# A two-layer image model on one core: the first and last rounds of a software pipeline in a written order, and scan matrices built by matrix products

## The chip, the cores and the metric

The kernel runs on one core of a Trainium2 chip. The core has a matrix engine (TensorE, PE in the profile; its weight loads are PEld), a vector engine (DVE), a scalar engine (ACT), GpSimd (POOL) and a queue for transfers (SyncE, SP). Each engine takes its instructions strictly in the order of the program, and waits for the others through semaphores. A matrix product can only write to PSUM, and has to be moved from there by DVE or ACT. The metric is the device time of one execution in microseconds (us); less is better.

## The reference

The input is 32 images of 56 x 56 pixels with 96 channels, in float32. Two layers follow each other; each adds a mixer and then a feed-forward network (FFN) to the running image, and each part begins with a normalization over the channels:

```python
x = x + _L0_conv_ref(_ln_c(x), ...)      # shifted 7x7-window attention, 3 heads of 32
t = _to_tokens(x)
t = t + _L0_ffn_ref(_ln_t(t), ...)       # 96 -> 384 -> 96, operands rounded to 8-bit floats
x = _from_tokens(t, x)
x = x + _L1_conv_ref(_ln_c(x), ...)      # gate * scan along the rows' axis, 192 channels
t = t + _L1_ffn_ref(_ln_t(t), ...)       # a second such FFN
```

The scan of layer 1 is a linear recurrence along one image axis with 16 states per channel:

```python
def step(state, u_w):
    st = state * A + u_w[..., None] * B
    y = jnp.sum(st * C, axis=-1) + S * u_w * D
    return (st, y)
```

As it is linear, its output is for each channel a fixed lower-triangular Toeplitz matrix (56 x 56) applied to a line of 56 pixels. The entries of the matrix are the channel's "taps": the sums over the states of C A^n B, with D added to the first.

## The kernel before

The images are cut into 128 blocks, four to an image; a block is 14 image rows of 56 pixels (seven tiles of 2 x 56 tokens and 96 channels) and lives in one of 14 buffers `xb` while everything is done on it. What is done to a block is some 90 steps with short names. In the order of a block's way:

| steps | what they do | engine |
|---|---|---|
| `LD` | load the block, six or nine transfers | SP |
| `sa`, `ma`, `na`; `ta`, `ea` | statistics, mean off, times root; transposes and their copy | DVE; PE, ACT |
| `q`, `k`, `v`; `eq`, `ek`, `ev` | projections (tiles `qk`, `pv`) and their copies | PE; ACT |
| `sc`; `st0`-`st2`; `ex0`-`ex2`; `av` | scores; scale and bias; exp; times values | PE; DVE; ACT; PE |
| `rc`, `an`; `tro`, `eo`; `pr`, `ad` | normalize; transpose, copy; output projection, add | DVE; PE, ACT; PE, DVE |
| `sf`, `mf`, `nf`, `tf`, `ef` | normalization of FFN 0 | DVE, POOL, POOL, PE, ACT |
| `hf`, `xf`, `rf`, `cf` (0-2); `yf`, `zf`, `bf`, `kf` | FFN 0: hidden product, copy, bias and relu, 8-bit cast; output product, copy, bias, add | PE, ACT, DVE, POOL/DVE; PE, ACT, DVE, POOL |
| `se`, `me`, `ne`, `te`, `xe` | normalization of the scan mixer | DVE, POOL, POOL, PE, ACT |
| `pu`, `th`, `uc` (0-3) | gate and expansion products; tanh; copy to `u` | PE; ACT; ACT |
| `SC`, `GA` (0-5) | scan as products with `toep` over the blocks of a window; gating | PE; DVE |
| `gt`, `eg`; `so`, `as` | transposes, copies; output product, add | PE, ACT; PE, DVE |
| `sg` ... `kg` | FFN 1, as FFN 0, with `cg` and `kg` on DVE | |
| `ST` | store the block, six or nine transfers | SP |

The eight steps `R0` to `R7` compute on DVE, in one pass, the inverse roots of all four normalizations that have statistics waiting; a normalization between `s` and `n` needs a full pass.

The order of the work is a text, `PIPELINED`: a list of entries `name:lag`. In round t the entry does its step on block t − lag, so the steps of about 14 blocks lie interleaved. The rounds run from t = 0 to 141; in the first ones only the entries of low lag have a block, in the last ones only those of high lag. `in_order` fixes this order on every engine. `banks` hands out four PSUM slots of two banks each, first in, first out; `EMPTIES` says which steps empty a slot.

Work that is done once (the preparation) is placed by hand around the first rounds: `prepare_attention` before round 0, `prepare_bias` after it, `prepare_hidden` and `prepare_matrices` around round 1, `prepare_mixer` before round 2. Much of it are memsets on POOL (L159 to L209, L267 and L439 to L475). `prepare_taps` (L276 to L301) raises the powers of A on DVE, weighs and sums them and transposes the taps on PE (tile `tapsT`). `load_toep` writes the taps 56 times to DRAM (L310) and reads them back in 12 transfers, shifted by one per line (L318), into the gate's second buffer `gts[1]`; `turn_toep` copies that, reordered, into `toep` before the first scan.

Before all this, `bounded` derives a flag from the attention's weights and position table; every engine reads it (L1065, L1066) and branches to the pipelined program or, where it does not hold, to a plain one (`IN_TURN`). With these inputs the pipelined one runs.

Of the kernel before, what the change touches and what calls it, by code (L numbers as in the profile page):

```python
# [17 lines left out]
C = 96  # L18
# [49 lines left out]

IN_TURN = (
    "LD:0 sa:0 R0:0 R1:0 R2:0 R3:0 R4:0 R5:0 R6:0 R7:0 ma:0 na:0 ta:0 ea:0 q:0 eq:0 k:0 ek:0 v:0 ev:0 any:0 "  # L70
# [8 lines left out]

EMPTIES = (  # L80
    "ea:ta eq:q ek:k ev:v st0:sc st1:sc st2:sc an:av eo:tro ad:pr ef:tf xf0:hf0 xf1:hf1 xf2:hf2 zf:yf xe:te "
# [6 lines left out]
def kernel(  # L88
# [81 lines left out]
    load(0)  # L170
    b1r = zeros(64, "bias1r")
    for iy in range(WS):
        nc.sync.dma_start(
# [7 lines left out]
    load(1)  # L181
# [36 lines left out]

    u = const.tile([128, EH, HW], F32, name="u")
# [8 lines left out]

    def bounded():
# [30 lines left out]
    abc = stage(C, 6 * NS).rearrange("p (n h s) -> p n h s", n=3, h=2)  # L260
    for n, src in enumerate((ssm_a, ssm_b, ssm_c)):
        nc.sync.dma_start(abc[:, n], src.rearrange("(h p) s -> p h s", p=C))
    a_t, b_t, c_t = abc[:, 0], abc[:, 1], abc[:, 2]
    d_t = const.tile([C, 2], F32, name="ssm_d")
    nc.sync.dma_start(d_t, ssm_d.rearrange("(h p) -> p h", p=C))
    for n in range(2, PRELOADED):
        nc.gpsimd.memset(xbufs[n], 0.0)  # L267
        load(n)
    powers = stage(C, 2 * HW * NS)
    powers = powers.rearrange("p (h t s) -> p h t s", h=2, s=NS)  # L270
    taps = stage(C, 4 * HW).rearrange("p (h t) -> p h t", h=2)
    taps_t = stage(2 * HW, E)
    ne = EH // 2

    def prepare_taps():
        nc.vector.tensor_copy(powers[:, :, 0, :], b_t)  # L276

        n = 1
        while n < HW:
# [8 lines left out]
            if n < HW:  # L288
                nc.vector.tensor_tensor(a_t, a_t, a_t, ALU.mult)
        nc.vector.tensor_tensor(powers, powers, c_t[:, :, None, :].to_broadcast([C, 2, HW, NS]), ALU.mult)  # L290
        nc.vector.memset(taps, 0.0)
        nc.vector.tensor_reduce(taps[:, :, HW:], powers, op=ALU.add, axis=AX.X)
        nc.vector.scalar_tensor_tensor(taps[:, :, HW], d_t, float(NS), taps[:, :, HW], op0=ALU.mult, op1=ALU.add)

        nc.vector.tensor_scalar_mul(taps, taps, 0.5)
        pt = banks("tapsT")
        for h in range(2):
            nc.tensor.transpose(pt[0 : 2 * HW, 0, h * C : (h + 1) * C], taps[:, h, :], ident[0:C, 0:C])

        for e0, src in ((0, 0), (ne, 3 * ne), (2 * ne, 2 * ne), (3 * ne, ne)):  # L300
            nc.vector.tensor_copy(taps_t[:, e0 : e0 + ne], pt[0 : 2 * HW, 0, src : src + ne])  # L301
# [817 lines left out]
```

## Time and profile before

| | us |
|---|---|
| runs shown: 3128.44, 3133.34, 3138.48; median | 3133.34 |
| the profiled execution's own time | 3137.61 |
| its span, first to last instruction | 3135.6 |
| PE, DVE, ACT, POOL busy | 3053.4, 2681.6, 2339.4, 1408.4 |
| start of R0 in rounds 2, 3, 6, 15 | 46.31, 66.03, 121.30, 305.62 |
| start of R0 in rounds 123, 130, 137 | 2845.04, 3007.13, 3098.08 |
| last `GA` ends; last `kg` ends | 3095.7; 3127.5 |

The profile is of one execution. "Busy" counts an engine's instructions, without waiting; a line such as L896 is a line of the kernel. In a row of the timeline stand the start, the duration, the engine, the line, the operation, output and input tiles, and in brackets the idle time before it with what ended it. The row "PEclk" and the clock in the stage tables are the clock that was granted to TensorE as a share of full speed. From round 18 (R0 at 375.51) to round 123 a round takes (2845.04 − 375.51) / 105 = 23.52 us.

### The profile page before, as it was taken

To read this page: it belongs to the slowest core of one execution; us is meant where nothing else is said; L and a number is where in the kernel's file an instruction comes from. 1 tells how busy PE (TensorE), PEld (TensorE's weight loads), DVE (VectorE), ACT (ScalarE), POOL (GpSimd) and SP (SyncE) were. 2 spreads that over 40 slices of the span, in tenths; PEclk is the share of its full clock that TensorE was granted. 3 is DMA by queue.
4 is the path that set the end of the run, shared out by engine and by line. 5 is a ranking of instruction groups with operands and counts; after the bars stand their busy time and mean duration, and the time that the engine had idled before them with its cause. 6 is when DMAs were issued, how large, how long until landed. Compare 5 with 4: busy or idle time off the path is not lost.

```text
span 3135.6 us, 180306 instructions
## 1 busy us (share of the span) xinstructions
PE 3053.4 (97%) x80164; PEld 2472.0 (79%) x80164; DVE 2681.6 (86%) x7213; ACT 2339.4 (75%) x4610; POOL 1408.4 (45%) x1091
## 2 busy tenths in 40 slices
PE   4999999999999999999999999999999999999996
PEld 3788888888888888888888888888888888888875
DVE  6778888888888888888888888888888888888886
ACT  1677777777777777777777777777777777777774
POOL 4454444444444444444444444444444444444441
PEclk8899999999999999999999999999999999999998
DMA  6100111111111111111111111111111111111001
GB/s 135 30 4 19 27 34 27 27 34 27 27 35 27 27 31 31 27 34 27 27 34 27 27 35 27 27 34 27 27 35 27 27 34 27 27 34 27 23 22 34
DMA packets 232640, 97.09 MB, mean 31 GB/s; under 512 B 225292, under 2 KB 231854, under 8 KB 231854
## 3 DMA queue, kind: packets, MB, share of 16 engines
q1 hardware_dynamic: 228410, 84.40, 11.7%
q8 instruction: 633, 10.37, 1.4%
q10 hardware_dynamic: 3444, 1.06, 0.2%
q14 instruction: 153, 1.25, 0.1%
HBM read 42.05 MB, written 43.35 MB: 27 GB/s over the span
## 4 chain that ended last, share of the span: by engine, by line
PE 96%; DVE 2%; POOL 1%; ACT 1%; issue 0%; SPq 0%; DMA 0%; ACTq 0%; POOLq 0%; DVEq 0%
PE pu L896 20%; PE so L992 10%; PE qk L616 9%; PE scan L939 6%; PE av L738 6%; PE pv L635 6%; PE ph_f L815 5%; PE s L658 5%; PE pr L793 5%; PE ph_g L815 4%; PE py_f L849 4%; PE py_g L849 4%; PE gt L217 3%; PE tr_a L217 2%; PE tr_f L566 2%; PE tr_e L217 2%
## 5 line engine op out<-in xcount | busy, mean ns | idle before, releaser
L896 PE MATMUL pu<-weg,xs 128*64 128x192 f32 x7168 | 663.3, 330 | 4.6 <-ACT xs L882 3.7
L535 DVE BATCH_NORM_STATS2 stats<-xb 128x6 f32<-128x192 f32 x2048 | 585.3, 346 | 1.7 <-POOL xb L871 1.6
L896 PEld LDWEIGHTS pu<-weg,xs 128*64 128x64 f32 x7168 | 485.6, 137 | 76.7 <-ACT xs L882 6.6
L839 POOL CAST hq<-h_f 128x784 fp8e5<-128x784 f16 x256 | 248.7, 972 | 497.6 <-DVE h_f L833 497.6
L555 POOL TENSOR_TENSOR xn_f<-xc_f,roots 128x672 fp8e5<-128x672 f32 x128 | 244.6, 1911 | 467.8 <-DVE roots L517 467.8
L871 POOL TENSOR_TENSOR xb<-xb,y_f 128x672 f32<-128x672 f32 x128 | 224.5, 1754 | 378.9 <-DVE y_f L867 375.6
L917 ACT COPY u<-pu 128x384 f32<-128x384 f32 (+1 forms) x512 | 236.4, 462 | 186.9 <-PE pu L896 186.9
L992 PE MATMUL so<-wso,gT 128*64 128x96 f32 x7168 | 326.7, 249 | 4.6 <-ACT gT L982 4.6
L827 ACT CAST h_f<-ph_f 128x784 f16<-128x784 f32 x384 | 318.2, 829 | 12.1 <-PE ph_f L815 12.1
L827 ACT CAST h_g<-ph_g 128x784 f16<-128x784 f32 x384 | 314.4, 821 | 13.6 <-PE ph_g L815 11.9
L992 PEld LDWEIGHTS so<-wso,gT 128*64 128x64 f32 x7168 | 302.6, 138 | 13.8 <-ACT gT L982 5.2
L541 POOL TENSOR_TENSOR xc_f<-xb,stats 128x672 f32<-128x672 f32 x128 | 174.8, 1365 | 288.0 <-DVE stats L535 170.5
L616 PE MATMUL qk<-xw,wqkv 128*32 128x196 f32 (+1 forms) x3072 | 296.2, 390 | 0.0
L687 DVE SCALAR_TENSOR_TENSOR pT<-s,bias 128x196 f32<-128x196 f32 (+1 forms) x512 | 213.5, 459 | 88.2 <-PE s L658 74.3
L628 ACT COPY qk<-qk 128x784 f32<-128x784 f32 (+1 forms) x256 | 166.1, 650 | 148.3 <-PE qk L616 146.5
L849 PEld LDWEIGHTS <-hq 128*128 128x128 fp8e5 x5376 | 252.7, 98 | 26.9 <-DVE hq L839 8.5
L959 DVE SCALAR_TENSOR_TENSOR gt<-gt,scan 128x448 f32<-128x448 f32 (+1 forms) x632 | 234.7, 428 | 35.4 <-PE scan L939 32.4
L700 ACT ACTIVATE pT<-pT 128x392 f32<-128x392 f32 x384 | 194.8, 528 | 74.2 <-DVE pT L687 74.0
L586 DVE TENSOR_TENSOR xb<-so,xb 128x384 f32<-128x384 f32 (+1 forms) x256 | 118.0, 502 | 152.4 <-PE so L992 152.4
L911 ACT ACTIVATE gt<-pu 128x384 f32<-128x384 f32 (+1 forms) x512 | 230.6, 450 | 18.0 <-PE pu L896 8.6
L616 PEld LDWEIGHTS qk<-xw,wqkv 128*32 128x32 f32 (+1 forms) x3072 | 120.6, 119 | 136.9 <-issue 127.6
L738 PEld LDWEIGHTS av<-v,pT 64*64 64x64 f32 x12288 | 193.4, 136 | 44.1 <-issue 33.3
(159 smaller groups left out, 6720.9 us busy)
## 6 DMA issues: line engine op xcount, KB each, us to landing
xb<-in_x_dram SPq DMA_DIRECT2D x224, 126.0 KB
out_dram<-xb SPq DMA_DIRECT2D x224, 126.0 KB
taps_d<-u SPq DMA_DIRECT2D x1, 4704.0 KB
xb<-in_x_dram SPq DMA_DIRECT2D x224, 13.1 KB
xb<-in_x_dram SPq DMA_DIRECT2D x224, 7.9 KB
out_dram<-xb SPq DMA_DIRECT2D x224, 13.1 KB
out_dram<-xb SPq DMA_DIRECT2D x224, 7.9 KB
xb<-in_x_dram SPq DMA_DIRECT2D x32, 72.0 KB
```

What stands on the lines that cost most here:

```text
L535: nc.vector.bn_stats(st[:, g : g + 2, :].rearrange("p g s -> p (g s)"), pair.rearrange("p g c -> p c g"))
L555: engine("n" + n).tensor_tensor(xn, xc, rs[:, :, None].to_broadcast([128, G, C]), ALU.mult, **saturate)
L616: nc.tensor.matmul(pq[j * rows : (j + 1) * rows, m, 0:size], wqkv[:, m * C + h0 * HD : m * C + h1 * HD], xws[i % 2][:, j * size : (j + 1) ...
L738: nc.tensor.matmul(po[r * 64 : r * 64 + 64, k, n0 : n0 + HD + 1], pT[kp, h, pair * W2 : pair * W2 + 64], v[kp, pair * NH + h, :], start=Tr ...
L815: nc.tensor.matmul(ph[:, half, 0:HALF], w1q[:, hc * 128 : (hc + 1) * 128], xqs[layer][:, half * HALF : (half + 1) * HALF], start=True, sto ...
L827: nc.scalar.copy(h16.rearrange("p (h t) -> p h t", h=2), held.pop(("ph", n, i, hc))[:, :, 0:HALF])
L839: engine(f"c{n}{hc}").tensor_copy(hq[:, :, 0:HW], h16.rearrange("p (r w) -> p r w", w=HW), saturate=False)
L849: nc.tensor.matmul(po[:, g - g0, :], hq[hc][:, 2 * g : 2 * g + 2, :].rearrange("p r w -> p (r w)"), w2q[:, hc, :], start=(hc == 0), stop=( ...
L896: nc.tensor.matmul(pu[h * RS : (h + 1) * RS, g, r * E : (r + 1) * E], xs[:, 2 * j + g, r, :], weg[:, h, :], start=True, stop=True,)
L917: nc.scalar.copy(dst, held["pu", i, j][:, 0:n, :, EH:].rearrange("p g r e -> p e g r"))
L959: nc.vector.scalar_tensor_tensor(part, part, 1.0, py[:, b, :, rows].rearrange("p e q -> p q e"), op0=ALU.add, op1=ALU.mult,)
L992: nc.tensor.matmul(po[r * ROW : (r + 1) * ROW, g, :], gT[:, h, 2 * g + r, :], wso[:, h, :], start=(h == 0), stop=(h == 1),)
```

## The change

The rounds 0 to 14 and those from 123 on are no longer generated from `PIPELINED`, but from two lists, `FILL` (994 entries, `name:block`) and `DRAIN` (1179 entries, blocks counted back from the end: −1 is the last). Between them `PIPELINED` runs as before for t = 15 to 122. The preparation is cut into named steps (`PREPARATION`) that stand in `FILL` among the others.

The scan matrices no longer go through DRAM. `delay` is a 56 x 120 matrix of shifted ones; for each of 56 offsets and two channel halves, `spread_taps` (steps `TB0` to `TB5`) multiplies a window of it with the taps, which puts the shifted taps on the right partitions in PSUM, and `turn_toep` (`TE0` to `TE5`) copies them into `toep`. The memset of `gts[1]`, the DRAM tile and its 13 transfers are gone, and the taps are kept without their leading zeros.

Some transfers change their queue: the position table's seven (`bias1r`) go from SP to ACT's queue, those of FFN 1 and of the scan mixer's weights from ACT's to SP, behind the loads of blocks 3 to 7. Block 1 and 2 are loaded directly after block 0, and A, B, C, D after block 2. One small exponential (`warm`) stands before the branch. Functions that are only cut into smaller ones (`prepare_taps` into `raise_powers`, `weigh_powers`, `sum_powers`, `transpose_taps`, `copy_taps`; `prepare_bias`, `prepare_ffn` and the fills likewise) are left out here.

```diff
+FILL_ROUNDS = 15
+DRAIN_ROUNDS = 5
+FILL = (
+    "sa:0 fh:0 R0:0 fa:0 T0:0 Bm:0 R1:0 Bp:0 R2:0 sa:1 R3:0 T1:0 Bc:0 R4:0 ma:0 R5:0 R6:0 R7:0 na:0 R0:0 "
+    "R1:0 T2:0 ta:0 Wf:0 ea:0 TQ:0 fi:0 v:0 q:0 T3:0 R2:0 k:0 ev:0 eq:0 ek:0 Cf:0 Tm:0 Tc:0 sc:0 Bd:0 st0:0 "
+    "sa:2 st2:0 st1:0 TB1:0 TB0:0 ex0:0 ex1:0 ex2:0 TB3:0 av:0 TE1:0 R3:0 ma:1 TB2:0 R4:0 TE3:0 R5:0 TE0:0 "
+    "R6:0 R7:0 na:1 rc:0 ta:1 an:0 tro:0 TE2:0 ma:2 ea:1 Wg:0 k:1 Cg:0 eo:0 pr:0 ad:0 sf:0 q:1 R0:0 R1:0 "
+    "mf:0 v:1 ek:1 R2:0 R3:0 eq:1 sc:1 TB4:0 ev:1 TB5:0 R4:0 st2:1 ex2:1 st0:1 st1:1 R5:0 R6:0 ex0:1 ex1:1 "
+    "av:1 R7:0 na:2 ta:2 nf:0 rc:1 TE5:0 tf:0 fx:0 an:1 ea:2 TE4:0 tro:1 k:2 ef:0 eo:1 sa:3 hf0:0 hf2:0 "
+    "xf0:0 ek:2 xf2:0 pr:1 fl:0 ad:1 sf:1 R0:0 q:2 eq:2 v:2 R1:0 ma:3 sc:2 R2:0 hf1:0 rf0:0 cf0:0 R3:0 st0:2 "
+    "st1:2 ev:2 st2:2 ex0:2 ex1:2 ex2:2 R4:0 R5:0 R6:0 xf1:0 rf2:0 R7:0 av:2 na:3 ta:3 rc:2 mf:1 nf:1 an:2 "
+    "ea:3 tf:1 rf1:0 tro:2 eo:2 cf2:0 cf1:0 v:3 sa:4 ef:1 yf:0 zf:0 ma:4 bf:0 ev:3 pr:2 kf:0 q:3 k:3 ad:2 "
...
+)
+DRAIN = (
+    "rf0:-9 xg1:-18 ad:-8 rg0:-18 ev:-7 sf:-8 q:-7 eq:-7 k:-7 te:-11 ek:-7 rg1:-18 se:-10 xe:-11 hf2:-9 "
...
+    "xg1:-4 R7:0 ng:-3 xg0:-4 yg:-5 tg:-3 zg:-5 sg:-2 xg2:-4 eg:-3 GA5:-1 ST:-8 R0:0 gt0:-1 gt1:-1 rg0:-4 "
+    "R1:0 bg:-5 R2:0 cg0:-4 R3:0 rg1:-4 rg2:-4 R4:0 cg2:-4 ST:-7 R5:0 hg0:-3 hg2:-3 eg0:-1 eg1:-1 kg:-5 "
+    "mg:-2 R6:0 cg1:-4 hg1:-3 ST:-6 so:-1 xg0:-3 xg2:-3 xg1:-3 R7:0 ng:-2 as:-1 yg:-4 sg:-1 rg1:-3 rg2:-3 "
+    "R0:0 tg:-2 zg:-4 R1:0 rg0:-3 eg:-2 R2:0 bg:-4 R3:0 kg:-4 R4:0 cg0:-3 R5:0 cg2:-3 mg:-1 R6:0 cg1:-3 "
+    "hg1:-2 hg0:-2 ST:-5 R7:0 xg0:-2 hg2:-2 xg2:-2 xg1:-2 ng:-1 rg2:-2 rg0:-2 rg1:-2 yg:-3 cg0:-2 tg:-1 "
+    "zg:-3 cg1:-2 eg:-1 bg:-3 hg0:-1 cg2:-2 kg:-3 xg0:-1 rg0:-1 hg2:-1 hg1:-1 xg2:-1 yg:-2 xg1:-1 rg2:-1 "
+    "cg0:-1 cg2:-1 ST:-4 zg:-2 rg1:-1 ST:-3 bg:-2 cg1:-1 kg:-2 yg:-1 zg:-1 bg:-1 kg:-1 ST:-2 ST:-1 "
+)
...
 EMPTIES = (
+    "Bc:Bp Cf:Wf Cg:Wg Tc:Tm TE0:TB0 TE1:TB1 TE2:TB2 TE3:TB3 TE4:TB4 TE5:TB5 "
...
     for n in range(2):
         nc.vector.memset(xbufs[n], 0.0)
-    load(0)
+        load(n)
     b1r = zeros(64, "bias1r")
     for iy in range(WS):
-        nc.sync.dma_start(
+        nc.scalar.dma_start(
...
-    load(1)
+    nc.gpsimd.memset(xbufs[2], 0.0)
+    load(2)
...
+    abc = stage(C, 6 * NS).rearrange("p (n h s) -> p n h s", n=3, h=2)
+    for n, src in enumerate((ssm_a, ssm_b, ssm_c)):
+        nc.sync.dma_start(abc[:, n], src.rearrange("(h p) s -> p h s", p=C))
...
-    for n in range(2, PRELOADED):
+    for n in range(3, PRELOADED):
         nc.gpsimd.memset(xbufs[n], 0.0)
         load(n)
...
-    def load_toep():
-        nc.sync.dma_start(taps_d.rearrange("w j e -> j w e"), taps_t[:, None, :].to_broadcast([2 * HW, HW, E]))
...
-    def turn_toep():
-        toep3 = toep[:, 0 : EH * HW].rearrange("p (e t) -> p e t", t=HW)
-        for e0, copy in ((0, nc.vector.tensor_copy), (EH // 2, nc.scalar.copy)):
-            part = slice(e0, e0 + EH // 2)
-            copy(toep3[:, part, :], gts[1][:, :, part].rearrange("p t e -> p e t"))
+    delay = const.tile([HW, HW + RS], F32, name="delay")
+    AT_ONCE = 5
+
+    def prepare_delays():
+        nc.gpsimd.memset(delay, 0.0)
+        for n in range(3):
+            nc.gpsimd.affine_select(
+                out=delay,
+                in_=delay,
+                pattern=[[1, HW + RS]],
+                compare_op=ALU.not_equal,
+                fill=1.0,
+                base=1 - (n + 1) * HW,
+                channel_multiplier=1,
+            )
+
+    def spread_taps(n):
+        held["toep", n] = pt = banks(f"toep_{n}")
+        for t in range(2 * AT_ONCE * n, min(HW, 2 * AT_ONCE * (n + 1))):
+            b, q = t // AT_ONCE % 2, t % AT_ONCE
+            steps = (t + SH) % HW + 1
+            for h in range(2):
+                nc.tensor.matmul(
+                    pt[h * RS : (h + 1) * RS, b, q * EH : (q + 1) * EH],
+                    delay[0:steps, HW - 1 - t : HW - 1 - t + RS],
+                    taps_t[0:steps, h * EH : (h + 1) * EH],
+                    start=True,
+                    stop=True,
+                )
+
+    def turn_toep(n):
+        pt = held.pop(("toep", n))
+        copy = nc.scalar.copy if n % 2 else nc.vector.tensor_copy
+        toep3 = toep[:, 0 : EH * HW].rearrange("p (e t) -> p t e", t=HW)
+        for b in range(2):
+            t0 = (2 * n + b) * AT_ONCE
+            t1 = min(HW, t0 + AT_ONCE)
+            if t0 < t1:
+                copy(toep3[:, t0:t1, :], pt[:, b, 0 : (t1 - t0) * EH].rearrange("p (t e) -> p t e", e=EH))
...
+        queue = (nc.scalar, nc.sync)[n]
...
+    warm = const.tile([1, 1], F32, name="warm")
+    nc.vector.memset(warm, 0.0)
+    nc.scalar.activation(warm, warm, AF.Exp)
     gam = const.tile([C, 1], F32, name="gam")
-    nc.scalar.dma_start(gam, gamma[:, None])
+    nc.sync.dma_start(gam, gamma[:, None])
...
-    def prepare_matrices():
-        fill(gts[1], 0.0)
...
+    preparation = dict(
+        fa=prepare_attention,
+        Bm=prepare_masks,
+        Bp=spread_bias,
+        Bc=copy_bias,
+        Bd=mask_bias,
+        fx=fill_inputs,
+        fh=lambda: fill_hidden(0),
+        Wf=lambda: turn_ffn(0),
+        Cf=quantize_first,
+        fs=fill_mixer,
+        fi=lambda: fill_hidden(1),
+        Wg=lambda: turn_ffn(1),
+        Cg=lambda: quantize_ffn(1),
+        fl=fill_loads,
+        T0=lambda: raise_powers(1, 16),
+        T1=lambda: raise_powers(16, HW),
+        T2=weigh_powers,
+        T3=sum_powers,
+        Tm=transpose_taps,
+        Tc=copy_taps,
+        TQ=prepare_delays,
...
+    def filled_and_drained():
+        yield from entries(FILL)
+        yield from rounds(PIPELINED, FILL_ROUNDS, nblocks - DRAIN_ROUNDS)
+        yield from ((name, nblocks + i) for name, i in entries(DRAIN))
...
     with tc.If(safe > 0) as branch:
-        pipeline(PIPELINED, True, b1T)
+        one_bias[0] = b1T
+        pipeline(filled_and_drained(), True)
```

## The prediction

> **What bounds the kernel now.** I read the page's engine shares and slices first, then the chain that ended last.
>
> ```profile
> PE 3053.4 (97%) x80164; PEld 2472.0 (79%) x80164; DVE 2681.6 (86%) x7213; ACT 2339.4 (75%) x4610; POOL 1408.4 (45%) x1091
> PE   4999999999999999999999999999999999999996
> PEclk8899999999999999999999999999999999999998
> PE 96%; DVE 2%; POOL 1%; ACT 1%; issue 0%; SPq 0%; DMA 0%; ACTq 0%; POOLq 0%; DVEq 0%
> ```
>
> TensorE is the bound except in the first and the last slice. The change rewrites only those ends, so next I cut the span into stages (columns: stretch, its length, then busy time of PE, PEld, DVE, ACT, POOL with instructions, the granted clock, DMA share, GB/s).
>
> ```profile
> 32.00:66.00 34.00, 23.01 (x368) 17.24 (x368) 21.58 (x60) 8.40 (x14) 0.00 (x0) 0.70 0.60 165
> 66.00:122.00 56.00, 46.32 (x1131) 35.06 (x1131) 37.58 (x100) 32.81 (x53) 23.93 (x16) 0.79 0.46 66
> 122.00:305.60 183.60, 183.60 (x5047) 147.70 (x5047) 145.01 (x404) 135.08 (x272) 89.66 (x67) 1.00 0.04 10
> 2845.00:3000.00 155.00, 155.00 (x4110) 126.39 (x4102) 131.97 (x356) 120.71 (x241) 71.47 (x55) 1.00 0.10 24
> 3000.00:3095.60 95.60, 84.71 (x1910) 68.20 (x1908) 79.54 (x220) 60.56 (x116) 29.28 (x23) 0.96 0.11 25
> 3095.60:3135.60 40.00, 18.60 (x218) 14.03 (x214) 25.33 (x83) 15.77 (x29) 2.66 (x2) 0.68 0.17 41
> ```
>
> PE is never idle between 122 and 3000 us: nothing can be won there. PE's idle time is 82.2 us (3135.6 − 3053.4): 29 before 32, 11.0 in 32–66, 9.7 in 66–122, 10.9 in 3000–3095.6 and 21.4 in the last 40 us. On top, wherever PE works in bursts its clock is granted at 0.5 to 0.8; taken in stretches of 4 us, busy time times the missing clock makes 12 us in 66–122 and 8 after 3000. These sums are all that the change can reach. Why PE starts late is in the timeline of the first 50 us:
>
> ```profile
> 16.51 4.63 DVE L451 CAST ident<-ident 128x112 fp8e5<-128x112 f32 x1
> 23.66 6.42 DVE L511 TENSOR_SCALAR roots<-variances 128x28 int32<-128x28 int32 x1
> 29.64 0.41 POOL L403 MEMSET w1q<- 128x384 fp8e5 x1
> 32.36 0.89 PE L217 MATMUL tr_a<-ident,xc_a 56*96 56x56 f32 x14 [16.87 <-DVE xc_a L555]
> 33.34 1.28 ACT L606 ACT_TABLE_LOAD   x1 [33.34 <-DMA xb<-in_x_dram]
> 42.51 0.54 PE L298 MATMUL tapsT<-ident,u 96*112 96x96 f32 x2 [4.40 <-DVE u L295]
> 44.10 4.34 PE L616 MATMUL qk<-xw,wqkv 128*64 128x392 f32 x24
> ```
>
> R1 (L511) has a median of 0.17 us over its 142 passes; here it took 6.42, until POOL's row of memsets ends at 30.05. Only then does block 0 get its root, and PE its first transposes. After `pv` (ends 38.1) PE waits again, for the taps, and `q` stands behind `tapsT` in its queue until 44.10.
>
> **The change, part by part.** FILL holds the same steps as rounds 0 to 14, DRAIN as rounds 123 to 141, each equally often, but for the root passes: 14 for 15, and 16 for 19. The steady rounds between are untouched. I go by the moved work.
>
> *Start.* POOL has no waits in its memsets, so it runs them in one row whatever FILL says; its length counts. Before R1 is free POOL now does: preamble and `xb` to 7.4 as now, `fh` 3.25, `fa` 3.05, `Bm` 1.25, `delay` (one memset and three selects, from the 128x128 rows at 0.20 and 0.29) 1.0, `fi` 4.4: 20.4. The 4.58 us memset of `gt` is gone; `xb` 8 to 13, `xq`, `xs` now follow `mf:0`, which waits. On DVE `T0` now stands before R1, and waits for B: SP issues the 6 loads of block 0 in 4.41 us from 1.66 and those of a block after it in 3.63, so three blocks and A, B end at about 14.2, and land about 1.9 later (as the last `bias1r`, issued by 11.6, released PE at 13.5): 16.1. T0 begins with a copy between SBUF tiles. If it is held like the cast of `ident` above, DVE goes on at 20.4; T0 1.9, R1, R2, R3, R4 0.9, `sa:1` 1.15, T1 1.9, `Bc` 1.3, `ma` 0.86, R5 to R7 0.66, `na` 0.86 make 9.5: `tr_a` at 29.9, 2.5 earlier. If nothing is held it is 25.8, 6.6 earlier; if B lands 2.5 us later than 20.4, 0. I take 2.5, as the two held rows lie nearest. The Trainium skill (SBUF — State Buffer, Who interferes with whom) has the port that DVE and GpSimd share locked for one whole instruction; by that rule DVE would wait for one memset (some 0.9 us) and `tr_a` come at about 26.7. The 6.42 us row outlasts ten memsets, so the rule falls short here.
>
> *Table load* at 33.34: now done by `warm`, before the branch, while ACT has nothing: 1.3 gained. *The taps* (T2, T3: 4.5 us of DVE behind `na:0`, done at 35) now come before PE needs them, and `q`, `k` follow `v` directly: 38.1 to 44.1, 6.0 gained. `Wf` (1.2 us of PE) lies beside `ea` (0.9). Lead at the first scores: 9.8 (7.3 to 13.9).
>
> *Toeplitz on PE.* 112 products of 96 columns are 224 PE instructions. The nearest row is pv, 32 instructions of 96 columns: 1.47 us in the steady rounds, 2.83 for the first block; so 46 to 88 ns each, 10.3 to 19.8 us. They stand between `sc:0` and `av:0` (60 products), around `tr_a` (20) and in block 1's softmax (32), where PE is idle now: 7.9 us between 48 and 84. With 15, the middle, for the price and 8 hidden, 7 are lost (2 to 16, with half of that cover gone). The skill (TensorE: Matmul & The Clock Gate, Part 1) says that some 3.4 us of activity release the clock; then all but the first would run at 46 ns, about 12 us in all, 4 lost. The products' evictions: at the old copies' rates (2.57 us for 2688 elements on DVE, 4.99 on ACT) 480 elements cost 0.46 and 0.9, six copies on each engine: together what the two old copies cost at 113 to 118. Left at 0, but on ACT they stand ahead of `ea:1`: at worst 2.
>
> *DRAM detour gone.* One write of 4.7 MB and 12 reads (SP 43.7 to 80) leave SP's queue, with the loads of blocks 8 on behind them; no wait of PE or DVE names them, so 0. `bias1r` (7 issues) moves from SP to ACT's queue: loads 1 and 2 start 4.7 us earlier, used above; `Bp` gets it by about 8.5. FFN 1's, gate's and `wso`'s 13 issues move from ACT to SP behind load 7: 28 + 6, landed by 36 us; `Wg` needs the first past 50. 0.
>
> *Rounds 3 to 5.* Now 55.3 us for 66–121, with 9.7 idle and 12 of clock missing. FILL puts FFN and mixer products of older blocks among the attention's waits, but a block's chain scores–softmax–av–projection–statistics–root remains, about 13 us at full clock against 18.4 us a round. Between 0 and 18 I take 10.
>
> Fill: 9.8 − 7 + 10 = 13 (from 7.3 − 18 + 0 = −11 to 13.9 − 2 + 18 = 30).
>
> *Drain.* Between 3000 and 3130 DVE is busy 104.8 us, PE 103.3; both have gaps, four PSUM slots couple them. Three passes fewer, 8 instructions 0.22 apart, are 5.3 us of DVE's chain. 99.5 us of DVE at the present density (104.8 busy in the 127.5 to the last `kg`, 82%) take 121 and give 6; at 90%, 111 and 17. The tail bounds it too: from the last `GA5` (3095.6) one block needs gt 0.9, eg 1.6, so 2.5, as 0.9, sg 1.1, root 1.8, ng 1.4, tg 0.7, eg 0.9, h 0.6, three x 2.4, r and c 0.9, yg 1.5, z b k 2.2, store 8.1: 27.5 for 40, but `hg` of four blocks shares DVE and ACT there. SP needs about 4 us for each store. I take 11 (4 to 20).
>
> Sum: 13 + 11 = 24. The profiled execution took 3137.6 (span 3135.6 and 2.0 around it), 4.3 over the median 3133.3 of the runs; from it 3113.6, from the median 3109.
>
> **Rivals.**
> *Toeplitz eats the fill.* For it: the clock is 0.5 in most 4 us stretches of 44–64. If all 224 run at 88 ns with 4 hidden, 16 are lost; with 4 in rounds 3 to 5, fill gives −2; with 9 of the drain, 7: 3126. Against: dense products are what the 1.00 rows have in common.
> *Ends packed to PE's limit.* Fill 28, drain 22: 3083. Against: the 27.5 us tail, and `tr_a` cannot start before 25.8.
> *Drain's order makes DVE wait* (the slower one). An order that opens a PSUM slot before its eviction stops an in-order engine. Its place is after 3000, its price is 99.5 us over DVE's density. It cancels the fill's 13 when those steps take 140.5 us where they take 127.5 now, at a density of 71%; at 63% they take 158, 30.5 more than now, and the kernel is 17 slower: 3151. For it: DVE is at 63% in the last 40 us already. Against: 83% in 3000–3095.6.
> *The change doesn't reach the time.* The first root waits for POOL as now, and later rounds absorb the lead as idle PE: 3133. Against it: PE has no idle time after 122, so a lead at 122 is kept to the end.
>
> **How the numbers follow.** Forecast 0.64 (its own range 3094 to 3122), Toeplitz 0.17, packed 0.06, DVE wait 0.09, no effect 0.04. A difference under 0.3% (9.4 us) can't be told from none here. Forecast and packed lie over it, Toeplitz in two fifths (0.07): faster 0.77; the rest of Toeplitz and half of no effect: same 0.12; DVE wait and the other half: slower 0.11. Range: gains of 48 to 6, 3085 to 3127, leaves the wait, the no-effect case and the packed one's edge out.
>
> **What would show it.** `tr_a` of block 0 at 28 to 30 with one long L720 or L425 row ending as POOL does, at about 20; no table load after the branch; first scores near 39; `toep` products at 46 or at 88 ns; R0 of the round after FILL near 292 instead of 305.6; steady rounds of 23.5 us; the last `GA` to the end in about 33 us, DVE denser than 82% after 3000. Wrong if steady rounds change, if POOL's row lasts past 25, or if waits of PE for evictions appear in the last 100 us.

## The result, and the profile after

The changed kernel takes 3108.69 us (median; 3107.67 to 3109.78), the kernel before in the same session 3133.41 us. The ratio is 0.9921 (95% interval 0.9904 to 0.9938), a gain of 24.7 us; the prediction said 24. The profiled execution of after took 3109.78 us with a span of 3107.9 us, that of before 3137.61 and 3135.6, so between the two traces lie 27.7 us.

The page of after: busy time, the slices of TensorE and of its clock, and the chain that ended last.

```profile
PE 3053.8 (98%) x80388; PEld 2483.2 (80%) x80388; DVE 2672.3 (86%) x7186; ACT 2338.1 (75%) x4616; POOL 1392.9 (45%) x1094
PE   6999999999999999999999999999999999999997
PEclk8999999999999999999999999999999999999998
PE 97%; DVE 2%; ACT 1%; POOL 1%; issue 0%; DMA 0%; POOLq 0%; ACTq 0%
```

Busy time of PE is what it was (3053.4 before), although 224 instructions have come in. Its idle time fell from 82.2 to 54.1 us (3107.9 − 3053.8). That difference, 28.1 us, is the whole gain. The stage table says where (stretch, length, busy time of PE, PEld, DVE, ACT, POOL with instructions, granted clock, DMA share, GB/s). The stretches are those shown of before, moved with the work: from the first `tr_a`, R0 of round 3, of round 6, to R0 of round 15; then from R0 of round 123, from 2990 (the place of 3000 before) to the last `GA`, and to the end.

```profile
26.50:57.40 30.90, 30.80 (x540) 26.02 (x542) 21.67 (x57) 11.14 (x18) 0.00 (x0) 0.72 0.12 26
57.40:109.30 51.90, 47.18 (x1203) 37.03 (x1201) 37.07 (x102) 28.88 (x54) 26.93 (x26) 0.84 0.16 38
109.30:295.90 186.60, 183.94 (x5075) 150.11 (x5071) 147.93 (x405) 133.82 (x272) 83.14 (x66) 1.00 0.04 10
2834.00:2990.00 156.00, 155.76 (x4101) 128.38 (x4089) 135.84 (x356) 121.03 (x241) 68.23 (x54) 1.00 0.10 23
2990.00:3074.00 84.00, 80.51 (x1906) 67.69 (x1903) 74.16 (x220) 60.47 (x117) 30.37 (x23) 1.00 0.12 28
3074.00:3107.90 33.90, 15.90 (x207) 11.76 (x207) 22.56 (x59) 15.18 (x28) 2.73 (x3) 0.73 0.21 49
```

| PE idle, us | before | after |
|---|---|---|
| to the first `tr_a` | 29 | 25 |
| to R0 of round 3 | 11.0 | 0.1 |
| rounds 3 to 5 | 9.7 | 4.7 |
| rounds 6 to 14 | 0 | 2.7 |
| last rounds, to the last `GA` | 10.9 | 3.7 |
| last `GA` to the end | 21.4 | 18.0 |

The starts of R0 give the same in time, as the lead over before:

| | before | after | lead |
|---|---|---|---|
| first `tr_a` | 32.36 | 26.51 | 5.9 |
| first scores | 48.4 | 33.8 | 14.6 |
| R0 of round 3 | 66.03 | 57.37 | 8.7 |
| R0 of round 6 | 121.30 | 109.28 | 12.0 |
| R0 of round 15 | 305.62 | 295.92 | 9.7 |
| R0 of round 123 | 2845.04 | 2834.04 | 11.0 |
| last `GA` ends | 3095.7 | 3074.0 | 21.7 |
| end of the span | 3135.6 | 3107.9 | 27.7 |

So in this pair of traces 11.0 us come from the first rounds and 16.7 from the last; 105 steady rounds took 23.5 us each as before. The changed kernel was profiled a second time, beside later experiments (span 3106.1): there R0 of round 3 comes at 56.79, of round 6 at 106.06, of round 15 at 293.02 and of round 123 at 2831.23. Two executions of the same kernel thus differ by some 3 us in such a row, and a smaller lead at one place of two traces shows little. The timeline of the first 60 us (start, duration, engine, line, operation, output and input, and in brackets the idle time before it with what ended it):

```profile
14.66 0.18 DVE L425 COPY u<-u 96x32 f32<-96x32 f32 x1 [4.17 <-DMA u<-in_L_conv_B_dram]
17.12 2.88 DVE L720 TENSOR_SCALAR roots<-variances 128x28 int32<-128x28 int32 x1
18.34 1.62 POOL L649 MEMSET gT<- 128x1024 f32 x2
26.51 0.89 PE L364 MATMUL tr_a<-ident,xc_a 56*96 56x56 f32 x14 [18.26 <-DVE xc_a L767]
31.23 2.38 PE L828 MATMUL qk<-xw,wqkv 128*64 128x392 f32 x24
33.82 1.62 PE L870 MATMUL s<-qk 32*64 32x49 f32 x96
35.23 7.17 PE L485 MATMUL toep<-u,delay 14*64 14x96 f32 x118
```

Three things are to be seen. T0's copy (L425) waited 4.17 us for B, but then ran in 0.18 us: it began in a break of POOL's row, whose memset of `delay` ends at 14.62 and whose first select starts at 14.69. R1 (L720) was held: it took 2.88 us, to the end of POOL's row (18.34 + 1.62 = 19.96). And from 26.5 on PE has no gap: `qk`, the taps, the scores and the products follow each other, where before PE waited 4.40 us for the taps.

### The profile page after: what moved, and what is told of

It is laid out like the page before. It is cut to its first block, busy times and chain, and to the rows that moved or that the text cites. A ratio compares the mean times of both kernels' runs of the same rounds, so it can differ in the third digit from the quotient of the medians.

```text
span 3107.9 us, 180524 instructions
## 1 busy us (share of the span) xinstructions
PE 3053.8 (98%) x80388; PEld 2483.2 (80%) x80388; DVE 2672.3 (86%) x7186; ACT 2338.1 (75%) x4616; POOL 1392.9 (45%) x1094
## 4 chain that ended last, share of the span: by engine, by line
PE 97%; DVE 2%; ACT 1%; POOL 1%; issue 0%; DMA 0%; POOLq 0%; ACTq 0%
PE pu L1108 20%; PE so L1204 10%; PE qk L828 9%; PE scan L1151 7%; PE av L950 6%; PE pv L847 6%; PE ph_f L1027 5%; PE s L870 5%; PE pr L1005 5%; PE ph_g L1027 4%; PE py_f L1061 4%; PE py_g L1061 4%; PE gt L364 3%; PE tr_f L778 2%; PE tr_a L364 2%; PE tr_e L364 2%
## 5 line engine op out<-in xcount | busy, mean ns | idle before, releaser
L1108 PE MATMUL pu<-weg,xs 128*64 128x192 f32 x7168 | 656.7, 330 | 2.0 <-issue 1.9
L767 POOL TENSOR_TENSOR xn_f<-xc_f,roots 128x672 fp8e5<-128x672 f32 x128 | 237.5, 1856 | 485.7 <-DVE roots L726 467.3
L899 DVE SCALAR_TENSOR_TENSOR pT<-s,bias 128x392 f32<-128x392 f32 (+1 forms) x512 | 214.5, 460 | 80.1 <-PE s L870 66.9
L950 PEld LDWEIGHTS av<-v,pT 64*64 64x64 f32 x12288 | 193.7, 136 | 38.3 <-issue 30.9
```

Of the source, the lines that this page charges most:

```text
L767: engine("n" + n).tensor_tensor(xn, xc, rs[:, :, None].to_broadcast([128, G, C]), ALU.mult, **saturate)
L950: nc.tensor.matmul(po[r * 64 : r * 64 + 64, k, n0 : n0 + HD + 1], pT[kp, h, pair * W2 : pair * W2 + 64], v[kp, pair * NH + h, :], start=Tr ...
L1108: nc.tensor.matmul(pu[h * RS : (h + 1) * RS, g, r * E : (r + 1) * E], xs[:, 2 * j + g, r, :], weg[:, h, :], start=True, stop=True,)
```

## Experiments on the last rounds

**The old order for the last rounds.** The rounds from 123 on come from `PIPELINED` again; all else is the changed kernel.

```diff
-        yield from rounds(PIPELINED, FILL_ROUNDS, nblocks - DRAIN_ROUNDS)
-        yield from ((name, nblocks + i) for name, i in entries(DRAIN))
+        yield from rounds(PIPELINED, FILL_ROUNDS, nblocks + 14)
```

> The changed kernel, with its last rounds (t = 123 to 141) generated from PIPELINED again instead of DRAIN. Theory (the written drain itself gains what the two traces differ by after the first pass of round 123, 290.6 - 273.9 = 16.7 us): about 3125, 16 to 17 over the changed kernel, with about 40 us from the last gating to the end instead of 33.9. Rival (the last stretch is shorter because of the state that the fill and the steady rounds leave behind): under 3115.

Measured: 3125.42 us, ratio to before 0.9966 (0.9953 to 0.9979) where the changed kernel has 0.9921: 14 us by the ratios. From R0 of round 123 to the end it takes 291.9 us in the traces, 18.0 more than with `DRAIN` (273.9) and 1.3 more than before (290.6); the profiled execution was the slowest of its eight, so the ratios are the better measure. The gain of the last rounds is the list's, and nothing else's. What is left, 0.9966, is the gain of the first rounds alone: 10.7 us.

**The old order without the last root passes.** As above, and the passes of rounds 139 to 141, which find no statistics, are left out.

```diff
-                    due = i >= 0
+                    due = 0 <= i < nblocks + 11
```

> As the first kernel of this call, but the root passes of rounds 139, 140 and 141, in which no normalization waits for a root, are left out. If the three passes fewer on VectorE are what the prediction's sum says (5.3 us of its chain): 4 to 5 us faster than the kernel with the old drain, 3120. Rival (only the order counts, the passes fill gaps that VectorE has anyway): within 1.5 us of it, 3124 to 3126.

Measured: 3124.06 us, ratio 0.9957 (0.9943 to 0.9970). The intervals of the two overlap; the medians lie 1.4 us apart, and from R0 of round 123 on the traces 2.9 (291.9 to 289.0). The stretches from the last `GA` on, of the first and of the second kernel:

```profile
3087.80:3127.50 39.70, 18.56 (x215) 13.28 (x212) 25.82 (x83) 15.88 (x29) 2.67 (x2) 0.65 0.17 42
```

```profile
3085.20:3122.90 37.70, 17.02 (x213) 12.53 (x210) 22.34 (x58) 15.88 (x29) 2.66 (x2) 0.74 0.18 44
```

DVE has 25 instructions and 3.5 us less work there, and the tail is 2.0 us shorter. With `DRAIN` it is 33.9. So the passes are worth some 1 to 3 us, which the ratios don't tell from nothing, and not the 5.3 that they occupy; the order itself is worth the rest, 11 us by the ratios (0.9957 to 0.9921). How it wins them shows in the longest wait of DVE from R0 of round 123 on (waiting instruction, releaser, us in all, times, longest): in before, in the changed kernel with the old order, and in the changed kernel.

```profile
DVE xb L586 <- PE so L992: 21.5, 15, 6.7
```

```profile
DVE xb L798 <- PE so L1204: 22.1, 15, 5.0
```

```profile
DVE xb L798 <- PE so L1204: 9.4, 11, 2.0
```

In the old order DVE stands for the scan mixer's output product (`so`) with other work behind it, with or without the other changes; `DRAIN` puts such work ahead of it. No run moves this one step alone, so its share of the 11 us isn't known. Between 2980 and 3100 us DVE is busy 105.5 of 120 us (88%), before 98.4 (82%).

## Experiments on the scan matrices

**The products twice.** Each product of `spread_taps` is done a second time.

```diff
-            for h in range(2):
+            for h in (0, 1, 0, 1):
```

> The changed kernel, with each of the 112 products that build the scan matrices done twice into the same place. Theory (on the path, half clock included): the pass of round 3 about 11 us later, the end 11 to 15 us later, 3120 to 3124. Rival (gaps absorb them): no more than 4 us later, under 3113.

Measured: 3124.13 us, ratio 0.9961 (0.9948 to 0.9974), that is 12.5 us by the ratios and 16.0 by the spans over the changed kernel. R0 of round 3 comes at 69.17, 11.8 later. A second set of products (a set keeps PE busy for 14.1 us in the changed kernel, at 48 to 91 ns each) is nearly all on the path; that the gaps of the first rounds take it up, the rival, is out. What this doesn't say is what the first set costs, since that one has the softmax waits to fill.

**The way through DRAM, first try.** `load_toep` (`Tl`) and `turn_toep` (`TO`) of before with the changed kernel's lists; the products are left out, and ACT zeroes `gts[1]` (`fg`).

```diff
-... Cf:0 Tm:0 Tc:0 sc:0 Bd:0 ... TB3:0 av:0 TE1:0 R3:0 ...
+... Cf:0 Tm:0 Tc:0 Tl:0 sc:0 Bd:0 ... av:0 fg:0 R3:0 ... st0:4 st2:4 TO:0 ...
```

> The changed kernel, with the scan matrices built through DRAM as before (taps written 56 times, read back shifted into the gate's second buffer, one copy on VectorE and one on ScalarE before the sixth round's root pass; the buffer is zeroed by ScalarE), the 112 products and their six evictions left out; everything else of FILL and DRAIN stays. Theory (TensorE is busy without a gap from 28 to 72 us, so the 14.2 us of products lie mostly on the path): the pass of round 3 at 50 to 53 instead of 57.4, the end 4 to 8 us earlier, 3101 to 3105. Rival 1 (the products fill gaps of TensorE): within 2 us of the changed kernel. Rival 2 (the large copies and the transfers stand in the way of block 4 and 5): slower than it, over 3112.

Measured: 3148.77 us, ratio 1.0038 (1.0027 to 1.0049). The zeroing stood behind the loads in the program, so it waited for them (and its zeros overwrote the matrices, so that the scan multiplied zeros):

```profile
ACT gt L466 <- DMA gt<-taps_d: 40.3, 1, 40.3
PE qk L819 <- ACT xw L809: 39.3, 1, 39.3
```

This run is no price for the products: the order was my mistake. It does show something else. PE stood still for 39.3 us from 44 us on. With no products to do, R0 of round 3 came 32.1 us late (89.51 for 57.37), R0 of round 15 34.7 us late (330.65), and the end 40.0 (3147.9 against 3107.9). So nothing of a delay in the first rounds was made up later.

**The way through DRAM, with the zeroing first.** The edit is shown against the first try.

```diff
-... sa:0 fh:0 R0:0 ... av:0 fg:0 R3:0 ...
+... sa:0 fg:0 fh:0 R0:0 ... av:0 R3:0 ...
```

> The changed kernel's two lists, but the scan matrices go the old way through DRAM, and the 112 products with their twelve copies are left out. `gts[1]`, into which they are loaded, is zeroed by ACT as FILL's second step, while ACT is idle (8.7 to 27.5), and not after its loads as in e3_dram_matrices; the reordering copy stands behind the scores of block 4. This prices the second half of the change by itself. Theory from e4_products_twice (a second set of products cost 11.8 us at R0 of round 3 and 13 to 16 at the end): all but a little of the products' 14.3 us is on the path, and DRAM's way costs nothing that is on it. Then R0 of round 3 is at 45 to 49 and the kernel takes 3096 to 3101, 7 to 12 us less than the changed kernel: by itself this half of the change is a loss. The prediction's own figure, 8 of 15 us beside other waits and 7 lost: 3101 to 3105. Rival: the transfers come too late or crowd out the loads, or PE only waits where the products stood: 3107 or more.

Measured: 3110.20 us, ratio 0.9916 (0.9904 to 0.9928): no different from the changed kernel (0.9921 and, in a second session, 0.9925). Yet R0 of round 3 came at 49.87, 7.5 us earlier; some 1.1 us of that lie ahead of the products, as POOL builds no `delay` and `tr_a` starts at 25.39. The lead is gone by round 6 (107.97 against 109.28 and, in the second profile, 106.06). Two stages of this run, with the columns as above, and a copy on ACT:

```profile
52.00:56.00 4.00, 1.92 (x81) 1.66 (x82) 2.99 (x8) 1.41 (x3) 0.86 (x1) 0.74 0.62 109
56.00:60.00 4.00, 4.00 (x101) 3.64 (x97) 2.25 (x6) 1.49 (x4) 3.88 (x6) 0.50 1.37 133
```

```profile
104.35 5.06 ACT L492 COPY toep<-gt 128x2688 f32<-128x2688 f32 x1
```

Where the products stood, PE now waits for the softmax (8.3 us in eight waits of `av` for `pT` in 28 to 126; 2.7 in three with the products), and after such a gap the clock is granted at 0.50. Rounds 3 to 5 take 58.1 us for 51.9: PE idles 7.4 us of them (4.7 in the changed kernel) at a mean clock of 0.77 (0.84). The reordering copy, in one piece of 5.06 us, holds ACT, and PE is busy for only 2.06 us from 108 to 112; but rounds 6 to 14 are no longer for it (187.0 us, 186.6 in the changed kernel). So in this order the two ways cost the same: the products take 7.5 us early, the old way gives as much back by round 6. How much of that is due to where I put the reordering copies stays open (DVE's half stands right ahead of R0 of round 6); other places weren't tried.

**The products in four parts.** Taps and `delay` stand on the lines 0 to 63 and again on 64 to 127; four products in a row use the four quarters of the array.

```diff
+        for q in range(AT_ONCE):
+            for b in range(2):
+                t = (2 * n + b) * AT_ONCE + q
...
-                    delay[0:steps, HW - 1 - t : HW - 1 - t + RS],
-                    taps_t[0:steps, h * EH : (h + 1) * EH],
...
+                for h in range(2):
+                    rows = slice((h ^ b) * RS, (h ^ b) * RS + steps)
...
+                        delay[rows, HW - 1 - t : HW - 1 - t + RS],
+                        taps_t[rows, h * EH : (h + 1) * EH],
...
```

> The same 112 products of the scan matrices, but taps and `delay` stand on the lines 0 to 63 and again on 64 to 127, and four products in a row use the four quarters of the 128 x 128 array, as the products of the scan itself do (64 instructions in 0.93 us, 14 ns apart). Theory: the products cost the time they take on PE (14.3 us, 48 to 91 ns each), because they are on the path; in quarters they run side by side and take 5 to 8 us, and the kernel gets 5 to 9 us faster than the changed kernel, less 0.5 to 1 for POOL's longer row (three more selects of some 0.25 and a memset). Rival one: products with different weights run one after another whatever lines they use: 14 us again, and 0 to 1 us slower. Rival two: they get short, but what PE wins it waits for the softmax of block 0 and 1: products 5 to 8 us, time within 2 us of the changed kernel. On the clock: if the half clock of 40 to 52 us comes from products that fill few lines and columns of the array, the stretch gets shorter or its clock higher; if it is the answer to PE's idle time before 26.5, it lasts as long as now.

For comparison the changed kernel ran once more beside this one:

> The changed kernel once more, beside the three that are compared with it. From its first runs (0.9921 of the kernel before, interval 0.9904 to 0.9938) I expect 0.991 to 0.9935, that is about 3108 to 3112 us; block 0's `tr_a` at 26.5, `toep` products 14.3 us in all, R0 of round 15 at 296.

It took 3108.11 us there (ratio 0.9925, 0.9912 to 0.9938). The four parts took 3102.43 us (0.9904, 0.9889 to 0.9918), 5.7 us less; the intervals overlap a little, but each of the four executions (up to 3105.55) is faster than each of the five beside them (from 3106.83). The first products of this run, and of each kernel a stretch at a clock of 0.50 (PE and PEld of the products alone, clock, DMA share, GB/s), first of the changed one:

```profile
34.61 4.92 PE L493 MATMUL toep<-u,delay 14*64 14x96 f32 x120 [1.51 <-DVE u L459]
```

```profile
38.24:42.18 3.94, 3.94 (x52) 3.71 (x49) 0.50 0.00 0
```

```profile
35.53:39.50 3.97, 3.97 (x97) 3.47 (x88) 0.50 0.14 30
```

That is 41 ns an instruction where the first 118 of the changed kernel took 61. Of those 118, though, most ran at a clock of 1.00 (72 in the 3.01 us to 38.24); at 0.50 an instruction takes 76 ns there and 41 here. All products together keep PE busy for 10.1 us in place of 14.1, more than I had hoped for (5 to 8), and R0 of round 3 comes 4.5 us earlier than in the run beside it (52.25 for 56.79). How much of that reaches the end is less sure: 5.7 us by the medians, 2.3 by the two spans (3103.8 and 3106.1), of which this run's is of its slowest execution. Over all products it is a gain of a third, at the same clock of nearly half, not of four times. What lets the clock fall isn't decided by it: it stays at 0.50 for 13.6 us here (35.5 to 49.2), but for as long in a later run with undivided products (36.6 to 50.3).

## Experiments on the start

**A shorter row on POOL.** The memsets of `hq` 3 to 5 and of `gT` move from `fi` to `fl`, behind `mf:0`.

```diff
     def fill_hidden(n):
-        for hq in hqs[3 * n : 3 * n + 3]:
-            fill(hq, 0.0)
+        if n == 0:
+            for hq in hqs[0:3]:
+                fill(hq, 0.0)
         fill(ffns[n][0], 0.0)
-        if n == 1:
-            for gT in gTs:
-                fill(gT, 0.0)
...
     def fill_loads():
...
+        for hq in hqs[3:6]:
+            fill(hq, 0.0)
+        for gT in gTs:
+            fill(gT, 0.0)
```

> The memsets of `hq` 3 to 5 (2.40 us) and `gT` (1.62 us) leave POOL's row before the first root and stand behind `mf:0`. My theory: R1 was held for 2.88 us at 17.12 by the rest of POOL's row (to 19.96), and PE's start is kept one to one to the end. Then POOL's row ends near 16.1, R1 takes 0.2 us, `tr_a` starts near 23.8 instead of 26.5, and the kernel is 2 to 3.5 us faster than the changed kernel (about 0.001 of the time). Rival: the lead is lost again before round 6, since the taps, the loads or the softmax of block 0 end the next waits: then R0 of round 6 stands where it does now (109.3) and the time differs by less than 1 us. A second rival: POOL has to do the 4 us later, beside block 0's normalization of FFN 0, and gives the gain back there: same or up to 2 us slower.

**R1 in another form.** POOL's row stays; R1 of the first two passes is written with a tile of constants (`root_bits`); the other passes keep theirs.

```diff
+    root_bits = const.tile([128, len(NORMS), G], F32, name="root_bits")
+    nc.vector.memset(root_bits, ROOT_BITS)
...
+        elif k == 1 and at == passes[k]:
+            nc.vector.scalar_tensor_tensor(
+                y.bitcast(I32), v.bitcast(I32), -0.5, root_bits, op0=ALU.mult, op1=ALU.add
+            )
         elif k == 1:
             nc.vector.tensor_scalar(y.bitcast(I32), v.bitcast(I32), -0.5, ROOT_BITS, op0=ALU.mult, op1=ALU.add)
```

> Only the first two root passes' R1 take another form of the same arithmetic: an instruction with two tensors and a scalar (as R0 and R3, which ran beside POOL's row in 0.17 to 0.19 us) instead of one tensor and two scalars. Theory: it is R1's form that is held by POOL's row, as the copy of T0 and R0 were not. Then R1 takes about 0.2 us at 17.1 although POOL's row still ends near 20, `tr_a` starts near 23.8 and the time is that of the shorter row, 2 to 3.5 us less than the changed kernel. Rival: whatever DVE has at that place is held by the memsets of 2.40 and 1.62 us: R1 ends at 20 again, `tr_a` at 26.5, the same time within 1 us.

Both did at their place what was expected. R1 took 0.17 us with the shorter row and 0.18 with the other form, and `tr_a` started at 24.00 and 23.88 instead of 26.55. Neither won time: 3110.19 (0.9931, 0.9919 to 0.9943) and 3111.53 (0.9933, 0.9920 to 0.9946) beside 3108.11. The first rival of the shorter row, a lead lost on the next wait, holds; the second, POOL's work coming later, isn't needed, as the other form leaves that work in place and wins no more. The timeline of the second run names the wait:

```profile
17.20 0.18 DVE L722 SCALAR_TENSOR_TENSOR roots<-variances,root_bits 128x28 int32<-128x28 int32 x1
34.20 0.15 DVE L643 TENSOR_SCALAR gam<-gam 96x1 f32<-96x1 f32 x1 [4.02 <-DMA gam<-in_L_conv_ln_gamma_dram]
34.72 10.03 PE L487 MATMUL toep<-u,delay 14*64 14x96 f32 x118 [2.26 <-DVE u L459]
```

`Cf` ends with a scaling of `gam`. The change moved the load of `gam` from ACT's queue to the sync queue, behind the loads of blocks 3 to 7. DVE, ready at 30.2, waits 4.02 us for it, with the copy of the taps queued behind; PE runs dry for 2.26 us, and the products begin at 34.7 as if nothing had been won. The run with the shorter row has the same wait (3.48 us), and so has the one with four parts (2.96).

**`gam` back on ACT's queue.** R1's other form, and this:

```diff
-    nc.sync.dma_start(gam, gamma[:, None])
+    nc.scalar.dma_start(gam, gamma[:, None])
```

> e9_other_root_form with one transfer moved back to ACT's queue: `gam`, which the changed kernel issues on the sync queue behind the loads of blocks 3 to 7 (29.98) and which Cf needs on DVE at 30.2; there DVE waited 4.02 us for it, and the taps' copy and with it the products behind that (PE idle 2.26 to 34.72). Theory: this wait took the 2.6 us that the earlier first root had won. Then DVE does not wait in Cf, the products start near 32.3 instead of 34.7, R0 of round 3 comes 2 to 3 us earlier than in the changed kernel (54 to 55 instead of 56.8 to 57.4) and the time is 2 to 3.5 us less (3104.5 to 3106.5). Rival: the lead is not lost there but in TensorE's clock (0.50 from 36 us on whenever the products start): products start earlier and take longer, R0 of round 3 within 1 us of 56.8 to 58.7, the same time.

Measured: 3106.39 us, ratio 0.9903 (0.9888 to 0.9917). Rows of this run:

```profile
30.24 0.14 DVE L643 TENSOR_SCALAR gam<-gam 96x1 f32<-96x1 f32 x1
33.18 6.79 PE L487 MATMUL toep<-u,delay 14*64 14x96 f32 x118
```

No wait is left before the scaling, the products begin 1.5 us earlier than without it, and R0 of round 3 comes at 53.80 (58.68 without, 56.79 in the changed kernel). To that place the theory holds, and its rival (a slower clock eats the lead) is out. Not all of it lasts: of the 4.9 us over the run without, 1.0 is left at R0 of round 15 (292.02 for 292.99), and the two spans end level (3104.6 and 3104.7). In time, the ratio lies 0.002, some 6 us, below the changed kernel's two, but the intervals overlap (up to 0.9917 here, from 0.9904 and 0.9912 there), so the sign is likely and the size isn't known.

**All together, and the root pass ahead of T0.** Four parts, R1's other form, `gam` on ACT's queue, and block 0's normalization before the step that waits for B. `T2`, `T3` and FFN 0's weights (`Wf`, `Cf`) move back as well; `Cf` now follows `st1:0` in the next line of the list:

```diff
-    "sa:0 fh:0 R0:0 fa:0 T0:0 Bm:0 R1:0 Bp:0 R2:0 sa:1 R3:0 T1:0 Bc:0 R4:0 ma:0 R5:0 R6:0 R7:0 na:0 R0:0 "
-    "R1:0 T2:0 ta:0 Wf:0 ea:0 TQ:0 fi:0 v:0 q:0 T3:0 R2:0 k:0 ev:0 eq:0 ek:0 Cf:0 Tm:0 Tc:0 sc:0 Bd:0 st0:0 "
+    "sa:0 fh:0 R0:0 fa:0 R1:0 Bm:0 R2:0 Bp:0 R3:0 R4:0 ma:0 R5:0 R6:0 R7:0 na:0 sa:1 T0:0 Bc:0 T1:0 R0:0 "
+    "R1:0 ta:0 ea:0 TQ:0 fi:0 v:0 q:0 T2:0 R2:0 k:0 ev:0 eq:0 ek:0 T3:0 sc:0 Tm:0 Wf:0 Tc:0 Bd:0 st0:0 "
...
```

> Three things together: the products in four parts (e6_four_parts), R1 of the first two passes in its other form and `gam` on ACT's queue (both as in e11_early_gamma), and block 0's root pass, mean and normalization before T0 in FILL, so that they no longer wait for B (4.2 us of idle DVE at 10.5 to 14.7). Theory: nothing but POOL's row and B held the first root. Then R1 follows R0 at 10.5, `xc_a` is normalized near 13.5, `tr_a` starts near 13.7 instead of 24.5 to 26.5, first scores near 23 to 25, and DVE's chain T1, T2, T3, Tc (to about 26 to 28) ends the wait of the products; of some 9 to 11 us of lead 4 to 8 remain at R0 of round 3 (52.25 in e6_four_parts, so 44 to 48) and at the end: 3093 to 3099. Rival: the lead is lost as in e5_short_pool_row, on what comes next (the loads of blocks 1 and 2 on the sync queue, FFN 0's weights, block 0's softmax behind T2 and T3): R0 of round 3 at 50 to 53, the time of e6_four_parts within 3 us (3100 to 3105).

Measured: 3097.41 us, ratio 0.9875 (0.9860 to 0.9889): 40 us less than the kernel before, 15 less than the changed one by the ratios, whose intervals lie apart. Its timeline:

```profile
10.41 0.19 DVE L730 SCALAR_TENSOR_TENSOR roots<-variances,root_bits 128x28 int32<-128x28 int32 x1
13.52 0.89 PE L366 MATMUL tr_a<-ident,xc_a 56*96 56x56 f32 x14 [5.26 <-DVE xc_a L781]
26.00 0.55 PE L456 MATMUL tapsT<-ident,u 96*128 96x96 f32 x2 [4.20 <-DVE u L451]
```

`tr_a` comes 13 us earlier than in the changed kernel, the scores 13.4, R0 of round 3 11.6 (45.74), the end 13.9 (3094.0 against 3107.9 in the spans). The scores came earlier than the theory had them (20.4 for 23 to 25); the rest is within what it gave. The run doesn't say what each of its parts is worth. PE now waits 4.20 us for T2 and T3 on DVE: that is the next end of the start, and it wasn't tried further.

## Why the prediction was right, step by step

*Start, 2.5 predicted, 5.9 measured.* R1 was held by POOL's row, which ended at 20.0 (20.4 predicted). Wrong was that T0's copy is held to the end of it. It ran at 14.66 in 0.18 us, so all of T0 was done before the row ended and fell out of the chain behind it. From R1's end to `tr_a` it took 6.5 us, not 9.5. The step that failed, "if it is held like the cast", was a choice between two rows of DVE that were both held to the end of something long. The trace of before had other rows: right behind that cast, six more ran through a row of POOL's memsets in 0.41 to 0.63 us each. The first of them, and the row:

```profile
21.18 0.55 DVE L404 CAST w1q<-w1t 96x384 fp8e5<-96x384 f32 x1
21.02 3.93 POOL L475 MEMSET xb<- 128x672 f32 x6
```

The free case of the same step is also 0.2 us off (16.1 and 9.5 make 25.6, not 25.8).

*First scores, 9.8 predicted, 14.6 measured.* To the start's extra 3.4 us came `qk` in 2.38 us instead of 4.34. No gap of PE lies ahead of it, and the clock is granted at 1.00 (31.4 to 33.6); before, PE was idle from 38.1 to 42.5, and `qk` ran at 0.50 (44.1 to 48.4). The table load is out of the way as said (7.38 to 8.66, ahead of the branch).

*Toeplitz products, 15 in all and 7 lost predicted.* Measured 14.1, and 7.5 at R0 of round 3 against the kernel without them (1.1 of it from the earlier `tr_a`). That 7 was met has some luck in it: the products' evictions, left at 0 from 0.46 us a copy on DVE, take 1.06 (median of six), as long as on ACT. That the way through DRAM costs 0 held for before, but not here: in the run that has it the seven microseconds are given back by round 6, so against its alternative this half of the change gains and loses nothing.

*Rounds 3 to 5, 10 predicted, 3.4 measured (6.0 in the second profile).* This is one of the two terms that were mis-sized most. Idle time fell by 5.0 us of 9.7, but PE still runs at a mean clock of 0.84 there (0.79 before), and the chain of a block from scores to root still ends some of the waits. Rounds 6 to 14, costed at nothing, lost 2.3 us (2.6): PE idles 2.7 us where the old order had no gap at all. Fill in sum: 13 predicted, 9.7 at R0 of round 15 and 11.0 at R0 of round 123 (12.6 and 13.8 in the second profile), and 10.7 by the ratio of the run with the old last rounds.

*Last rounds, 11 predicted, 16.7 measured.* The tail from the last `GA` was right (33 predicted, 33.9). Ahead of it 10.7 us were won. The failed step is that DVE's work goes on "at the present density" of 82% (81% to the last `kg`, where DVE is busy 103.5 us, not 104.8). It went to 88%, close to the other value that was worked out (90%, and a gain of 17). The root passes, which carried 5.3 us of the 11, are worth 1 to 3.

*Moved transfers, 0 predicted.* True of the changed kernel: DVE reaches `gam` at 32.9, when it has landed. But "`Wg` needs the first past 50" named the wrong user. `Cf` needs `gam` at 30, and any earlier start runs into it.

*Sum.* 24 predicted, 27.7 between the traces (2 less than said in the first rounds, 5.7 more in the last) and 24.7 between the medians, as the profiled execution of before lay 4.3 us above its median and that of after 1.1. So the sum came out right with terms that were off in both directions, and that it did is luck. Of the rivals, "Toeplitz eats the fill" would have needed 16 lost; "ends packed" (3083) wasn't reached even with the start rewritten (3097); DVE's waits from R0 of round 123 on fell from 43.3 to 30.6 us (the rows of that view added) instead of rising; and a lead at 122 us did stay: it is 12.0 us at R0 of round 6 and 11.0 at R0 of round 123, and the failed run was 33.4 us late at the one and 39.2 at the other.

## What to carry to other kernels

An engine that is busy from a certain point to the end turns most of what is won ahead of that point into time, and what is lost too; so read the first rounds wait by wait. When one wait is removed there and nothing comes of it, look up what ends the next one before giving up the idea: here a load of 96 numbers, moved to a longer queue, held up the products, so that nothing of an earlier start was left at R0 of round 3. Work that has to be done once is best costed against the gaps it can fill and against the other way of doing it, and not by its own length.

## What the runs showed of the hardware

*Half clock without a gap.* A stretch of the changed kernel, columns as in the stage table:

```profile
38.24:55.30 17.06, 17.06 (x272) 15.08 (x269) 9.41 (x21) 6.94 (x11) 0.00 (x0) 0.50 0.01 2
```

The clock stands at 0.50 for 17 us while PE has work in every microsecond: products of 14 to 56 lines, `av`, transposes. It is back at 1.00 4 us after the next projections begin (`qk` at 51.3). With the products done twice it stays at 0.50 from 38.3 to 65.6 us, again without a gap. So it lasts longer with more of this kind of work. Which property of it counts (lines used, columns, weight loads) wasn't separated. The Trainium skill (TensorE: Matmul & The Clock Gate, Part 1) has the clock released by some 3.4 us of activity. This stretch contradicts that, if a row of small products counts as activity; the prediction's figure by that rule, 12 us for the products, was 2 too low.

*Who is held by a row of POOL's instructions.* Three kinds are seen at the same place. R1 in its other form (0.18 us at 17.20) and R0 (0.19 at 10.30) ran beside a memset without a delay. T0's copy of 96 x 32 is held for no more than the one instruction that POOL has in progress: in the second profile of the changed kernel it ends at 15.00, just behind POOL's select (14.69 to 14.97), and in both runs through DRAM just behind a memset that ends at 15.31, with more memsets following.

```profile
14.77 0.23 DVE L425 COPY u<-u 96x32 f32<-96x32 f32 x1 [4.86 <-DMA u<-in_L_conv_B_dram]
14.69 0.28 POOL L467 TENSOR_SCALAR_AFFINE_SELECT delay<-delay 56x120 f32<-56x120 f32 x1
```

R1 with one tensor and two scalars was held for 2.88 us, through four memsets. In the run with four parts it came at 17.48, took 0.52 us and ended with the memset in progress (17.13 + 0.84), though five more followed; in the runs through DRAM it took 1.47 and 1.48, to the end of the second and last memset. The Trainium skill (SBUF — State Buffer, Who interferes with whom) names `tensor_scalar` among the forms that can take the port shared with GpSimd, and has the loser wait for one whole instruction. The first agrees with these runs; the second fits the copy and one of the R1 rows, and in the others the wait outlasted several. Why it ended after one memset in one run and not in another stays open.
